# A fused attention block on one core: query and key biases carried in the first row of the weights

## The chip, the cores and the metric

The kernel runs on one core of a Trainium2 chip. Its engines work in parallel, each through its own instructions in order: TensorE (PE, with its weight loads as PEld), VectorE (DVE), ScalarE (ACT), GpSimd (POOL) and SyncE (SP), which here only issues transfers. The metric is the device time of one execution in microseconds. Three runs of the kernel before took 2831.59 to 2832.27 us, median 2831.97.

## The reference

The input is 4 batches of 1024 tokens, 512 wide. A layer norm over the 512 values gives `xn`. From it come queries, local keys and local values of 16 heads of 128 (`xn @ W + b` with `Wq`, `Wlk`, `Wlv`). Queries and keys go through an RMS norm and a rotation. Each query looks at a window of the last 128 tokens, and at the best 8 of the compressed entries (one for every 4 tokens); the mean of both goes through `Wo`. A float8 product of `xn` with `input2` and the input itself are added.

```python
xn = _layernorm(x, axis=-1)
q = (hidden_states @ Wq + bq).reshape(Bq, Sq, NH, D).transpose(0, 2, 1, 3)
q = apply_rope(rmsnorm(q, qn_w), pos)
lk = apply_rope(rmsnorm((hidden_states @ Wlk + blk).reshape(Bq, Sq, NH, D).transpose(0, 2, 1, 3), kn_w), pos)
...
merged = (ctx_sparse + ctx_local) * 0.5
x = x + (merged @ Wo + bo) + _L0_ffn_ref(xn, L0_ffn_input2, L0_ffn_scale, L0_ffn_scale1)
```

The layer norm has no weights of its own, so the 512 values of a token's `xn` sum to zero, but for rounding.

## The kernel before

The 4096 tokens are 32 blocks ("chunks" in the code) of 128 tokens, 8 to a batch. A block is done in 8 units of two heads. One loop (L791) runs over all 256 units; `s` is the unit, `t` its block and `u` its place in the block. The order on every engine is the order in which the loop body issues, written out by hand. All weights stay in SBUF.

In iteration `s` the body issues, in this order:

- the scores of unit `s` (L563: window keys, entries and a mask product on TensorE), and `keep_context` of `s-2` (ScalarE);
- `weigh` (L592) of both heads: masks, top-8 and replacement on VectorE, exponentials on ScalarE;
- `queries` (L440) of unit `s+3`: four products of 128x512 that give queries and keys of two heads (`qp`), and a fifth, in bfloat16, that adds the biases through a selecting column;
- `settle` (L623) on VectorE: choice, sums and scaling of the sparse weights;
- a first step of the generators in `running`, then the squares of `s+3` (ScalarE, L296) and from them `r`, a power on GpSimd (L290, L291);
- `settle_window` (ScalarE, L643), `to_output` of `s-2`, and a second step of the generators;
- from unit 8 on `turn` (L654): two transposes into `probB` on VectorE and a transfer to DRAM; then `values_of` (`s+1`), `normalize` (L461) of `s+3` (`th` on VectorE, a rotation half on GpSimd, `rb`, L309), the value products of `s-1`, `fetch` of the turned weights (`probT`), `turn_keys` of `s+3` with its transfers (`qk`, `qT`, `lkT`) and `keep_values` (ScalarE).

The first eight units turn weights and keys on TensorE instead (`turn_here`, `keep_turned`); their iterations also round `input2` to float8 values (units 0 to 3) and load the later weights.

Two generators run beside this, each by two steps in an iteration. `chunk_prep` of block `t+2` starts in unit 7 of block `t`: statistics (unit 7), `xn` (unit 0), its transposes `xp` and the copy `xnT` (unit 1), the product with `Wk`, `Wv` and `Wcmp` with the softmax over four tokens (units 2 and 3), entries (units 4 to 7, with a small rotation, L404 and L308, in unit 6). `chunk_eight` of block `t` starts in unit 5: `quantize` (L255) has three passes on VectorE (`qv_x`, `qm_x`) and an addition on GpSimd (L267) in its first step, then a GpSimd pass in each of the next three; the float8 product `fp` follows on TensorE in unit 7, and `f` and its addition to the input in that unit's second step.

PSUM tiles of tag `pp` (`xp`, `yp`, `ep`, `cp` of the entries, `fp`, `vp`, `tp`) share two buffers, and `scratch` (`xn`, `y`, `qv`, `qm`, `f`) shares two in SBUF. Each output of a block is finished by `x_sum` (L762) in unit 1 of the next block.

Of the kernel before, what the change touches and what calls it, by code (L numbers as in the profile page):

```python
# [12 lines left out]
F32 = mybir.dt.float32  # L13
BF16 = mybir.dt.bfloat16
U32 = mybir.dt.uint32
AF = mybir.ActivationFunctionType
ALU = mybir.AluOpType
AX = mybir.AxisListType

P = 128  # L20
# [18 lines left out]
def kernel(  # L39
# [26 lines left out]
    nc = tc.nc  # L66
    B, S, HID = hidden.shape
    NH = Wq.shape[1] // D
    KK = HID // P
    NCH = S // P  # L70
    NU = NH // 2
    NE = P // RATIO
    NT = B * NCH
# [12 lines left out]
    def scratch(name, shape=(P, 512), dtype=F32):  # L86
        return work.tile(list(shape), dtype, tag="scratch", name=name, bufs=2)
# [157 lines left out]
    def late_constants():  # L245
# [6 lines left out]
        nc.tensor.transpose(bp[:, 0:NH], blv_n, ident[:NH, :NH])  # L252
        nc.scalar.activation(blvT, bp[:, 0:NH], AF.Copy, scale=0.5)

    def quantize(dst, src, scalar, tag, m=None):  # L255

        v = scratch(f"qv_{tag}") if tag[0] == "x" else src
        if m is None:  # L260
            m = scratch(f"qm_{tag}")
        nc.vector.tensor_scalar(v, src, scalar, None, ALU.mult)
        nc.vector.tensor_scalar(
            m.bitcast(U32), v.bitcast(U32), 0x7F800000, None, ALU.bitwise_and
        )
        nc.vector.tensor_scalar(m, m, FP8_MIN_NORMAL, 1.5 * 2.0**20, ALU.max, ALU.mult)
        nc.gpsimd.tensor_tensor(v, v, m, ALU.add)  # L267
        yield
        nc.gpsimd.tensor_tensor(v, v, m, ALU.subtract)
        yield  # L270
        nc.gpsimd.tensor_scalar(m, v, FP8_OVERFLOW, 0.0, ALU.mult, ALU.mult)
        yield
        nc.gpsimd.tensor_tensor(dst, v, m, ALU.add)
        yield
# [43 lines left out]
    def chunk_prep(t):  # L318

        b, c = divmod(t, NCH)  # L320
        xt = x_tiles.pop(("norm", t))
        if c == 0:
            entries[b] = (
                work.tile([P, 2 * P], F32, tag="ckT", name=f"ckT_{b}"),
                work.tile([P, 2, D], F32, tag="cv", name=f"cv_{b}"),
            )
        ckT, cv = entries[b]
        st = work.tile([P, 8], F32, tag="lnst", name=f"lnst_{t}")
        nc.vector.bn_stats(st[:, 0:6], xt)
        nc.vector.bn_aggr(st[:, 6:8], st[:, 0:6])  # L330
        r = rstd_of(st[:, 7:8], 1, 1.0, EPS_LN, f"lnr_{t}")
        yield "A0"
        if c == 0:
            nc.gpsimd.memset(cv, 0.0)
        yield "B0"
        xn = scratch(f"xn_{t}")
        nc.vector.tensor_scalar(xn, xt, st[:, 6:7], r, ALU.subtract, ALU.mult)
        yield "A1"
        yield "B1"
        xp = pp(f"xp_{t}")  # L340
        for k in range(KK):
            nc.tensor.transpose(xp[:, ts(k, P)], xn[:, ts(k, P)], ident)
        yield "A2"
        xnT = work.tile([P, KK, P], F32, tag="xnT", name=f"xnT_{t}")
        nc.scalar.copy(xnT.rearrange("p k s -> p (k s)"), xp)
        chunks[t] = xnT
        yield "B2"


        yp = pp(f"yp_{t}")  # L350
        for k in range(KK):
            nc.tensor.matmul(
                yp[:, 0 : 2 * D + 1],
                xnT[:, k, :],
                wkv_sb[:, k, :],
                start=(k == 0),
                stop=(k == KK - 1),
            )
        yield "A3"
        y = scratch(f"y_{t}")[:, 0 : 2 * D + 1]  # L360
        nc.scalar.copy(y[:, 0 : 2 * D], yp[:, 0 : 2 * D])
        nc.gpsimd.memset(y[:, 2 * D : 2 * D + 1], 1.0)
        nc.vector.tensor_scalar(
            logits[:, 0:1], yp[:, 2 * D : 2 * D + 1], bcmp_sb, None, ALU.add
        )
        row = work.tile([P, 2, BLK], F32, tag="row", name=f"row_{t}", bufs=1)
        red = work.tile([P, BLK // RATIO], F32, tag="red", name=f"red_{t}", bufs=1)
        nc.vector.transpose(row[:, 0, :], logits)
        fours = row[:, 0, :].rearrange("p (n r) -> p n r", r=RATIO)
        nc.vector.tensor_reduce(red, fours, AX.X, ALU.max)  # L370
        nc.vector.tensor_tensor(
            fours, fours, red.unsqueeze(2).to_broadcast([P, BLK // RATIO, RATIO]), ALU.subtract
        )
        nc.scalar.activation(row[:, 0, :], row[:, 0, :], AF.Exp)
        yield "B3"
        yield "A4"
        spread_w = work.tile([P, NE], F32, tag="spread", name=f"spread_{t}", bufs=1)
        nc.vector.transpose(row[:, 1, :], row[:, 0, :])
        nc.vector.tensor_scalar(spread_w, picks, row[:, 1, 0:1], None, ALU.mult)
        yield "B4"  # L380
        ep = pp(f"ep_{t}")
        nc.tensor.matmul(ep[0:NE, 0 : 2 * D + 1], spread_w, y, start=True, stop=True)
        yield "A5"
        total = work.tile([NE, 1], F32, tag="total", name=f"total_{t}", bufs=1)
        kv = work.tile([NE, 2, D], F32, tag="kv", name=f"kv_{t}", bufs=1)
        nc.vector.reciprocal(total, ep[0:NE, 2 * D : 2 * D + 1])
        nc.vector.scalar_tensor_tensor(
            kv.rearrange("p h d -> p (h d)"),
            ep[0:NE, 0 : 2 * D],
            total,  # L390
            bkv_sb,
            ALU.mult,
            ALU.add,
        )
        yield "B5"
        g, o = divmod(c * NE, P)
        nc.scalar.copy(cv[o : o + NE, g, :], kv[:, 1, :])
        ess = work.tile([NE, 1], F32, tag="ess", name=f"ess_{t}", bufs=1)
        square_sum(ess, kv[:, 0, :], f"e{t}")
        er = rstd_of(ess, 1, 1.0 / D, EPS_RMS, f"er_{t}")  # L400
        ck = kv[:, 0:1, :]
        yield "A6"
        yield "B6"
        nc.vector.scalar_tensor_tensor(  # L404
            ck[:, 0, :], ck[:, 0, :], er, norm_w[0:NE, 1, :], ALU.mult, ALU.mult
        )
        ra = work.tile([NE, ROPE], F32, tag="ra_e", name=f"ra_e{t}", bufs=1)
        rotate(ck, angles[t][1], 1, ra, f"e{t}")
        yield "A7"
        yield "B7"  # L410
        cp = pp(f"cp_{t}")
        nc.tensor.transpose(cp[:, 0:NE], ck[:, 0, :], ident[:NE, :NE])
        yield "A8"
        nc.vector.tensor_copy(ckT[:, ts(c, NE)], cp[:, 0:NE])  # L414
        yield "B8"

    def chunk_eight(t):

        xt, xnT = x_tiles["sum", t], chunks[t]
        x8 = work.tile([P, KK * P], BF16, tag="x8", name=f"x8_{t}", bufs=1)  # L420
        src = xnT.rearrange("p k s -> p (k s)")
        yield from quantize(x8, src, scales[:, 0:1], f"x_{t}")
        fp = pp(f"fp_{t}")
        for k in range(KK):
            nc.tensor.matmul(
                fp, x8[:, ts(k, P)], w2_sb[:, k, :], start=(k == 0), stop=(k == KK - 1)
            )
        yield
        f = scratch(f"f_{t}")
        nc.vector.scalar_tensor_tensor(f, fp, inv, bo_sb, ALU.mult, ALU.add)  # L430
        nc.gpsimd.tensor_tensor(xt, xt, f, ALU.add)
# [8 lines left out]
    def queries(n):  # L440
        t, u = place(n)
        xnT = chunks[t]
        qp = psum.tile([P, 512], F32, tag="qp", name=f"qp_{n}")
        for k in range(KK):
            nc.tensor.matmul(qp, xnT[:, k, :], wqk_sb[u][:, k, :], start=(k == 0), stop=False)  # L445
        nc.tensor.matmul(
            qp, sel[:, u : u + 1].to_broadcast([P, P]), bias_b, start=False, stop=True
        )
        ss = work.tile([P, 4], F32, tag="ss", name=f"ss_{n}")
        units[n] = {"qp": qp, "ss": ss}  # L450

# [326 lines left out]
    def for_unit(n, *todo):  # L778
        if 0 <= n < NN:
            for f, *more in todo:  # L780
                f(n, *more)
# [9 lines left out]
    for s in range(-3, NN + 2):  # L791
        t, u = place(s)
# [2 lines left out]
            running = [*running[-2:], chunk_prep(t + 2)]  # L795
        if u == 3 and 0 <= t < NT:
            load_x(t, "sum")
        if u == 5 and 0 <= t < NT:
            running = [*running[-2:], chunk_eight(t)]
        if u == 4 and 0 <= t and t + 2 < NT:  # L800
            load_x(t + 2, "norm")
# [32 lines left out]
        if s + 3 >= NU:  # L834
            for_unit(s + 3, (turn_keys,), (fetch_keys,))
        for_unit(s + 1, (keep_values,))
        if s < NU:

            if s == -1:
                late_constants()  # L840
                for k in range(KK):
                    nc.scalar.dma_start(w2_raw[k], input2[ts(k, P), :])
            if 0 <= s < KK:
                for _ in range(4):
                    next(rounding, None)
            if 3 <= s + 6 < NU:
                load_wqk(s + 6, nc.scalar)
            if 3 <= s + 4 < NU:
                load_wlv(s + 4, nc.scalar)
            if 0 <= s + 1 < NU:  # L850
                load_wo(s + 1, nc.scalar)
# [49 lines left out]
```

## Time and profile before

| what | value |
|---|---|
| median of 3 runs | 2831.97 us |
| the profiled execution | 2833.53 us |
| its span, first to last instruction | 2831.6 us |
| mean granted TensorE clock | 0.997 |
| busy: PE, DVE, ACT, POOL | 2769.0, 2247.1, 1299.1, 821.3 us |
| products of `queries` (L445), busy | 945.5 us |
| transfers, mean | 141 GB/s |

Busy time is the time in which an engine has an instruction at work; idle time before an instruction is put down to what ended it. A row of the time line gives start, duration, engine, line, operation and tiles, a count where several rows are merged, and in brackets the idle time before it with its cause. Rows of one engine overlap by some tenths of a microsecond, so what an instruction costs its engine is the distance to the next start, and not its duration. Some matmul rows are missing from the trace: of the 256 bias products it has 59, while all 256 of their weight loads are there.

### The profile page before, as it was taken

The numbers are of one execution on the slowest core, as the hardware profiler recorded it, in microseconds if no ns is written. First come the engines' busy times: TensorE is split into PE (matmuls) and PEld (weight loads), VectorE is DVE, ScalarE is ACT, GpSimd is POOL, SyncE is SP. The second block draws the span as 40 slices with busy tenths as digits, with TensorE's granted clock in tenths as the row PEclk, the third lists the DMA queues.
The fourth block names the chain that finished last, engine by engine and source line by source line (L and its number), as shares of the span: only waits on it lengthen the run. The fifth ranks groups of instructions, "written<-read, shape, count | busy, mean of one in ns | idle before, by whom it ended". The sixth has DMA issues, their size and how long they took to land. (4 is left out here: it accounts for less than half of the span.)

```text
span 2831.6 us, 48506 instructions
## 1 busy us (share of the span) xinstructions
PE 2769.0 (98%) x12771; PEld 1873.8 (66%) x12969; DVE 2247.1 (79%) x9132; ACT 1299.1 (46%) x5075; POOL 821.3 (29%) x1161
## 2 busy tenths in 40 slices
PE   6999999999999999999999999999999999999998
PEld 4666666666666666666666666666666666667666
DVE  5777888888777778888877787888887777888886
ACT  3445444444444454444444444444444444444443
POOL 3432232322233322233223333223222233322221
PEclk9999999999999999999999999999999999999999
DMA  7345455555445445555544444555554544555553
GB/s 230 90 138 138 133 143 152 144 150 153 127 124 139 137 133 152 144 151 149 149 126 131 134 135 134 155 148 149 146 149 122 135 136 131 136 152 155 143 149 108
DMA packets 620850, 399.85 MB, mean 141 GB/s; under 512 B 306880, under 2 KB 573984, under 8 KB 620576
## 3 DMA queue, kind: packets, MB, share of 16 engines
q1 hardware_dynamic: 608352, 383.18, 48.8%
q10 hardware_dynamic: 12224, 13.56, 1.5%
q8 instruction: 105, 1.72, 0.3%
q14 instruction: 169, 1.38, 0.2%
HBM read 212.53 MB, written 184.03 MB: 140 GB/s over the span
## 5 line engine op out<-in xcount | busy, mean ns | idle before, releaser
L445 PE MATMUL qp<-wqk,xnT 128*128 128x512 f32 x2048 | 945.5, 604 | 4.9 <-DMA scales<-in_L_ffn_scale_dram 3.3
L445 PEld LDWEIGHTS qp<-wqk,xnT 128*128 128x128 f32 x2048 | 370.6, 191 | 385.2 <-issue 371.5
L612 ACT ACTIVATE prob<-sc,neg 128x256 f32<-128x256 f32 (+1 forms) x512 | 236.0, 461 | 779.6 <-DVE taken L611 759.3
L537 PEld LDWEIGHTS vp<-wlv,xnT 128*128 128x128 f32 x2048 | 386.5, 190 | 188.7 <-issue 94.0
L537 PE MATMUL vp<-wlv,xnT 128*128 128x256 f32 x2048 | 487.0, 381 | 17.2 <-DVE ckT L414 11.9
L753 PE MATMUL op<-wo,cT 128*128 128x512 f32 x1024 | 484.9, 596 | 7.1 <-ACT cT L735 1.5
L290 POOL TENSOR_SCALAR r<-ss 128x4 f32<-128x4 f32 x256 | 49.8, 194 | 1067.3 <-ACT junk L296 1059.3
L661 DVE STREAM_TRANSPOSE probB<-prob 128x512 f32<-128x512 f32 (+2 forms) x494 | 282.4, 609 | 92.5 <-ACT prob L643 89.1
L467 DVE SCALAR_TENSOR_TENSOR th<-qp,r,norm_w 128x128 f32<-128x128 f32 x1024 | 283.6, 339 | 71.0 <-POOL r L291 70.2
L309 POOL TENSOR_TENSOR rb<-th,cs 128x256 f32<-128x256 f32 x256 | 247.0, 965 | 278.0 <-DVE th L467 277.9
L296 ACT ACTIVATE junk<-qp 128x128 bf16<-128x128 f32 x1024 | 284.1, 277 | 88.0 <-remote 42.7
L549 ACT COPY lv<-vp 128x256 f32<-128x256 f32 x256 | 95.5, 373 | 477.6 <-PE cp L720 420.0
L753 PEld LDWEIGHTS op<-wo,cT 128*128 128x128 f32 x1024 | 188.9, 190 | 188.4 <-issue 113.9
L720 PE MATMUL cp<-probT,lv 128*128 128x128 f32 x1920 | 299.4, 276 | 4.4 <-DMA probT<-pr 4.4
L720 PEld LDWEIGHTS cp<-probT,lv 128*128 128x128 f32 x1920 | 276.1, 193 | 18.1 <-issue 5.2
L291 POOL TENSOR_TENSOR r<-r,nhalf 128x4 f32<-128x4 f32 x256 | 259.6, 1014 | 21.4
L720 PE MATMUL cp<-probT,cv 128*128 128x128 f32 x1536 | 256.7, 276 | 0.0
L582 PE MATMUL sc<-ckT,qT 128*128 128x96 f32 (+7 forms) x1024 | 226.5, 303 | 0.0
L643 ACT ACTIVATE prob<-prob,tot 128x256 f32<-128x256 f32 (+1 forms) x512 | 223.0, 484 | 3.6 <-DVE tot L637 3.6
L720 PEld LDWEIGHTS cp<-probT,cv 128*128 128x128 f32 x1536 | 214.3, 193 | 0.0
L605 DVE CUSTOM_DVE_ANT_0 sc<-sc,mask_b 128x256 f32<-128x256 f32 (+1 forms) x512 | 202.6, 396 | 7.2 <-PE sc L583 6.6
L579 PE MATMUL sc<-lkT,qT 128*128 128x128 f32 x1024 | 207.8, 285 | 0.0
(123 smaller groups left out, 3858.3 us busy)
## 6 DMA issues: line engine op xcount, KB each, us to landing
pr<-probB SPq DMA_DIRECT2D x127, 512.0 KB, 2.6
probT<-pr SPq DMA_DIRECT2D x508, 128.0 KB, 2.9
qk<-thb SPq DMA_DIRECT2D x992, 64.0 KB, 2.0
pr<-probB SPq DMA_DIRECT2D x96, 384.0 KB, 2.6
probT<-pr SPq DMA_DIRECT2D x384, 96.0 KB, 2.4
qT<-qk SPq DMA_DIRECT2D x248, 128.0 KB, 2.3
lkT<-qk SPq DMA_DIRECT2D x248, 128.0 KB, 2.5
x_norm<-_attn_hidden_states_dram SPq DMA_DIRECT2D x32, 256.0 KB, 3.2
```

The costliest lines, as they stand in the source:

```text
L291: nc.gpsimd.tensor_tensor(r, r, nhalf[: ss.shape[0], 0:n], ALU.pow)
L296: nc.scalar.activation(junk[: src.shape[0]], src, AF.Square, accum_out=acc)
L309: nc.gpsimd.tensor_tensor(bb, x12, wide(cs[:, HALF:ROPE]), ALU.mult)
L445: nc.tensor.matmul(qp, xnT[:, k, :], wqk_sb[u][:, k, :], start=(k == 0), stop=False)
L467: nc.vector.scalar_tensor_tensor(th[:, i, :], qp[:, ts(i, D)], r[:, i : i + 1], norm_w[:, i // 2, :], ALU.mult, ALU.mult,)
L537: nc.tensor.matmul(vp[:, 0:256], xnT[:, k, :], wlv_sb[u][:, k, :], start=(k == 0), stop=(k == KK - 1),)
L582: nc.tensor.matmul(sc[:, spa], q, ckT[:, 0:m], start=True, stop=False)
L612: nc.scalar.activation(prob[:, loc], sc[:, loc], AF.Exp, bias=neg[:, 0:1], scale=-1.0, accum_out=tot[:, 0:1],)
L643: nc.scalar.mul(prob[:, loc], prob[:, loc], tot[:, 0:1])
L661: nc.vector.transpose(pb[:, :, ds(h * g, g), :], prob[:, parts[0] * P : (parts[-1] + 1) * P].rearrange("p (g b i) -> p b g i", b=NB, i=BLK),)
L720: nc.tensor.matmul(blocks(cp[:, h, :]), v, probT[:, :, h * len(parts) + i - parts[0], :], start=(i == parts[0]), stop=(i == parts[-1]),)
L753: nc.tensor.matmul(op, cT[:, h, :], wo_sb[u][:, h, :], start=(u == 0 and h == 0), stop=(u == NU - 1 and h == 1),)
```

## The change

The biases are no longer added by a product of their own, from block 1 on. As the values of `xn` sum to zero, subtracting the first row of `Wq` and `Wlk` from all their rows leaves the product as it is and makes the first row zero. While block 0 is in work, iteration `s` does this for the weights of unit `s`: one VectorE subtraction over 128x2048, with the row spread over the partitions by a transfer into `probB`'s memory. Then the biases are written into the empty row by two transfers of 1 KB. The token side needs a one at that place: `xnT` gets a fifth block, a copy of the first whose first row is set to one, and blocks from 1 on use it for the first of the four products. Block 0 keeps the bias product.

As the sum must now be zero more exactly, the mean is taken off twice: ScalarE subtracts it in place and sums what is left, and `xn` subtracts the mean of that. `xn` moves a step later within unit 0. The float8 generator starts in unit 6 and not in unit 5, so its product and `f` fall in unit 0 of the next block.

```diff
+    first_row = {}
+    def load_first_row(u):
+        row = work.tile([P, 1024], F32, tag="probB", name=f"first_row_{u}", bufs=1)[:, 0:512]
+        for i, w in enumerate((Wq, Wlk)):
+            nc.sync.dma_start(row[:, ts(i, 256)], w[0, ts(u, 256)].partition_broadcast(P))
+        first_row[u] = row
+    def fold_first_row(u):
+        w = wqk_sb[u]
+        nc.vector.tensor_tensor(
+            w, w, first_row.pop(u).unsqueeze(1).to_broadcast([P, KK, 512]), ALU.subtract
+        )
+        for i, bias in enumerate((bq, blk)):
+            nc.sync.dma_start(
+                w[0:1, 0, ts(i, 256)], bias[ts(u, 256)].partition_broadcast(1)
+            )
...
         yield "B0"
+        off = work.tile([P, 2], F32, tag="off", name=f"off_{t}")
+        nc.gpsimd.tensor_scalar(off[:, 0:1], st[:, 6:7], -1.0, None, ALU.mult)
+        nc.scalar.activation(
+            xt, xt, AF.Identity, bias=off[:, 0:1], scale=1.0, accum_out=off[:, 1:2]
+        )
+        nc.gpsimd.tensor_scalar(off[:, 1:2], off[:, 1:2], 1.0 / HID, None, ALU.mult)
+        yield "A1"
         xn = scratch(f"xn_{t}")
-        nc.vector.tensor_scalar(xn, xt, st[:, 6:7], r, ALU.subtract, ALU.mult)
-        yield "A1"
+        nc.vector.tensor_scalar(xn, xt, off[:, 1:2], r, ALU.subtract, ALU.mult)
         yield "B1"
...
-        xnT = work.tile([P, KK, P], F32, tag="xnT", name=f"xnT_{t}")
-        nc.scalar.copy(xnT.rearrange("p k s -> p (k s)"), xp)
+        xnT = work.tile([P, KK + 1, P], F32, tag="xnT", name=f"xnT_{t}")
+        nc.scalar.copy(xnT[:, 0:KK, :].rearrange("p k s -> p (k s)"), xp)
+        if t:
+            nc.scalar.copy(xnT[:, KK, :], xp[:, 0:P])
+            nc.vector.memset(xnT[0:1, KK, :], 1.0)
...
-            nc.tensor.matmul(qp, xnT[:, k, :], wqk_sb[u][:, k, :], start=(k == 0), stop=False)
-        nc.tensor.matmul(
-            qp, sel[:, u : u + 1].to_broadcast([P, P]), bias_b, start=False, stop=True
-        )
+            nc.tensor.matmul(
+                qp,
+                xnT[:, k if k or not t else KK, :],
+                wqk_sb[u][:, k, :],
+                start=(k == 0),
+                stop=(t > 0 and k == KK - 1),
+            )
+        if not t:
+            nc.tensor.matmul(
+                qp, sel[:, u : u + 1].to_broadcast([P, P]), bias_b, start=False, stop=True
+            )
...
-        if u == 5 and 0 <= t < NT:
+        if u == 6 and 0 <= t < NT:
             running = [*running[-2:], chunk_eight(t)]
...
         for_unit(s + 1, (keep_values,))
+        if 0 <= s < NU:
+            fold_first_row(s)
+        if 0 <= s + 1 < NU:
+            load_first_row(s + 1)
```

More of the change, by code (lines that the diff above doesn't have):

```diff
@@ L420, in chunk_eight @@
         x8 = work.tile([P, KK * P], BF16, tag="x8", name=f"x8_{t}", bufs=1)
-        src = xnT.rearrange("p k s -> p (k s)")
+        src = xnT[:, 0:KK, :].rearrange("p k s -> p (k s)")
         yield from quantize(x8, src, scales[:, 0:1], f"x_{t}")
```

## The prediction

> **What bounds the kernel now.** I read the page first, then the list of waits, then the time line of TensorE, and last one steady token block unit by unit. A unit is two heads of a block of 128 tokens; eight make a block, 32 blocks the kernel.
>
> ```profile
> PE 2769.0 (98%) x12771; PEld 1873.8 (66%) x12969; DVE 2247.1 (79%) x9132; ACT 1299.1 (46%) x5075; POOL 821.3 (29%) x1161
> ```
> TensorE works 98% of the span. The removed product's price is the distance of starts:
>
> ```profile
> 1525.72 3.68 PE L445 MATMUL qp<-wqk,xnT 128*128 128x512 f32 x8
> 1529.24 0.38 PE L446 MATMUL qp<-bias_b,sel 128*128 128x512 bf16 x1
> 1529.45 0.60 PE L342 MATMUL xp<-ident,xn 128*128 128x128 f32 x4
> ```
> The row says 0.38, but the next product starts 0.215 us later (0.215 to 0.216 wherever a transpose or an output product follows it). 248 of 256 go: 53.4 us.
>
> That is a gain only if nothing else is nearly as slow. Below are units 1, 5 and 6 of block 4 and the sum of its eight, as VectorE walks them (first local mask L605 to that of the next unit):
>
> ```profile
> 391.30:401.91 10.61, 10.61 (x55) 7.53 (x55) 8.79 (x35) 5.33 (x20) 2.17 (x3) 1.00 0.60 174
> ...
> 435.26:447.51 12.25, 12.20 (x60) 8.46 (x61) 9.60 (x37) 5.67 (x22) 5.77 (x7) 1.00 0.47 130
> 447.51:458.28 10.77, 10.72 (x52) 7.49 (x52) 9.38 (x39) 4.86 (x19) 4.32 (x6) 1.00 0.51 148
> ...
> sum 88.22, PE 87.66 PEld 60.38 DVE 72.44 ACT 40.96 POOL 25.18; mean PE 10.96 PEld 7.55 DVE 9.05 ACT 5.12 POOL 3.15
> ```
> Columns: stretch, length, then busy time of PE, weight loads, DVE, ACT, POOL, the granted clock (1.00), DMA. TensorE idles 0.56 of 88.22 us; VectorE has 15.8 idle. Is that room? The waits say whom it waits for:
>
> ```profile
> ACT prob L612 <- DVE taken L611: 759.3, 488, 4.7
> ...
> DVE th L311 <- POOL rb L309: 159.1, 256, 0.6
> ...
> DVE probB L661 <- ACT prob L643: 89.1, 120, 1.5
> ...
> DVE th L467 <- POOL r L291: 70.2, 92, 3.2
> ...
> DVE logits L363 <- ACT y L361: 57.2, 31, 5.9
> DVE x_sum L762 <- PE op L753: 43.4, 32, 6.6
> ```
> Nearly all are waits for ScalarE or GpSimd, which themselves wait for VectorE (first line). So there is a ring: mask and top-8 (DVE), exponentials, squares, window scaling (ACT), r (POOL), th (DVE), rb (POOL), th, next unit. Only x_sum, and squares that find their product unfinished, wait for TensorE. In block 4 I take these out: without x_sum's 0.77 us and ScalarE's gaps of 0.20, 0.73 and 0.45 us ahead of the squares in units 2 to 4, units 1 to 4 are 0.56, 0.29, 0.82 and 0.61 us shorter (each then runs from its exponentials on without a gap). The ring alone then takes 85.9 us, TensorE 87.7. The same over blocks 1 to 30 (128.68 to 2734.41 us, 86.86 a block): ring 84.15. **VectorE's ring is within 3% of being the bound**; what the change adds to it decides.
>
> **The change part by part.** Block 4 is the worked case.
>
> *Bias products:* TensorE needs 87.66 - 8 x 0.2155 = 85.9 us. The move of the float8 product out of unit 7 also ends the wait there of vp for a bank that VectorE empties (ckT, 11.7 us over 17 blocks, 0.39 a block): mean need 86.86 - 1.72 - 0.39 = 84.75.
>
> *Float8 rounding from unit 5 to unit 6.* Today in unit 5:
>
> ```profile
> 440.83 0.43 DVE L266 TENSOR_SCALAR qm_x<-qm_x 128x512 f32<-128x512 f32 x1
> ...
> 441.40 1.27 POOL L267 TENSOR_TENSOR qv_x<-qv_x,qm_x 128x512 f32<-128x512 f32 x1 [0.57 <-DVE qm_x L266]
> ...
> 442.75 0.20 POOL L290 TENSOR_SCALAR r<-ss 128x4 f32<-128x4 f32 x1
> ...
> 444.08 1.12 DVE L467 SCALAR_TENSOR_TENSOR th<-qp,r,norm_w 128x128 f32<-128x128 f32 x4 [0.83 <-POOL r L291]
> ```
> L267 stands ahead of r on GpSimd, so th starts 2.82 us after qm_x ends. Without it unit 5 falls back to its squares (late by the cv copy and junk_e, 0.8): 12.2 to 10.95, -1.24. Unit 6 has the kv rotation ahead (L404 to L312, 1.43 us); then 1.39 of rounding ends at 7.38 us into the unit and th starts at 10.20, not 7.33: +2.85. The trace holds this very pile-up once, in block 0, where kv work falls in unit 5:
>
> ```profile
> 100.18 0.33 DVE L404 SCALAR_TENSOR_TENSOR kv<-kv,er,norm_w 32x128 f32<-32x128 f32 x1
> ...
> 102.17 0.43 DVE L266 TENSOR_SCALAR qm_x<-qm_x 128x512 f32<-128x512 f32 x1
> ...
> 105.42 1.13 DVE L467 SCALAR_TENSOR_TENSOR th<-qp,r,norm_w 128x128 f32<-128x128 f32 x4 [2.50 <-POOL r L291]
> ```
> Again 2.82 us after qm_x. Unit 7 keeps its length without f (0.74): its th waits for r behind lnr, not for f.
>
> *Second centring, unit 0.* ScalarE's 128x512 pass stands ahead of the squares. Rows: L612 takes 0.368 us at 128 columns, 0.474 at 256, so 0.69 at 512. ScalarE has no gap there in block 4, and f moves into this unit beside it: +0.69. Bounds: 0 (f and xn alone), 0.88 (with an accumulator read of 0.19). GpSimd's two 128x1 steps (0.19 each, as lnr's first) fit before r and ahead of xn.
>
> *Extra copy and row of ones, unit 1.* The memset waits on VectorE for ScalarE's copy and holds probB and th behind it:
>
> ```profile
> 396.70 0.69 DVE L762 TENSOR_TENSOR x_sum<-x_sum,op 128x512 f32<-128x512 f32 x1 [0.77 <-PE op L753]
> 396.98 0.57 ACT L345 COPY xnT<-xp 128x512 f32<-128x512 f32 x1
> ```
> xnT ends 6.25 us into the unit (probB starts at 6.00 today, at 397.30); a 128-column copy adds 0.17 (0.27, from 0.373 at 256 and 0.572 at 512, less 0.10 overlap), the memset 0.15 (rows: 0.06 at 4 columns, 0.27 at 256). probB can start at 6.6 against 5.4 for the ring alone: +1.16. Bounds +0.6 (x_sum waiting as now) to +1.4.
>
> Block 4: 85.91 + 0.69 + 1.16 - 1.24 + 2.85 = 89.37, against 88.22 now and 85.9 for TensorE. So the ring takes over. Done alike for blocks 1 to 30: +0.4 to +1.2 each, -0.4 in blocks 8, 16, 24; ring 87.48, **sum +18.6**.
>
> *Folding, block 0.* One 128x2048 subtraction per unit ends each unit on VectorE. TENSOR_TENSOR rows: 0.425 us at 256 columns (L310), 0.69 at 512 (L762); on that line 2.25 at 2048, bounds 2.1 and 2.75. In block 0 TensorE already waits for VectorE (vp for the lkT copy, 1.60 and 1.38 us) and VectorE's masks never for TensorE, so nothing hides it: 18.0. The rounding's move is -3.2 + 2.2 there, the first memset +0.3: **+17.2**. The 16 row loads and 16 bias loads on SP wait for a fold and are needed 10 and 50 us later; the queue's typical landing is 2 to 3 us, so 0. What stands behind them on SP, qk from unit 5 on, waits no longer than the fold.
>
> *Start.* xn now follows pass 0.69, GpSimd 0.2, and ScalarE's first pass starts only after the table load (10.55): first product at 14.1 for 11.19, **+2.9** (bounds 1.2, as the second product waits for weights until 19.86 anyway, and 3.5).
>
> *End.* Block 31 has no kv work: ring 10.5 a unit where TensorE took 10.92, for five units, and unit 5's probB 0.9 earlier: **-4**.
>
> Sum: 2.9 + 17.2 + 18.6 - 4 = +34.7 on the profiled 2833.5 (span 2831.6 and 1.9 around), 2868; on the median of 2831.97, which stands 1.6 lower: **2867**.
>
> [...] VectorE is 82% busy in block 4 (72.44 of 88.22), yet its ring leaves 2.3 us. [...]
>
> **Rivals.** (1) TensorE stays the bound, the other side: -53.4 - 11.7 + 2.9 + 14.3 (block 0 less 3 us of lead) = -48, 2784. It decides if the ring grows by under 0.6 us a block (84.15 to 84.75) where I find 3.3. For it: 98% busy. Against: the 2.82 us chain seen twice. (2) The additions on ScalarE hide (units 0 and 1 cost nothing): ring +1.61, a block 1.1 shorter than now; -33 + 16 = -17, 2815. For it: x_sum's wait stands just there. Against: x_sum no longer waits once TensorE leads. (3) TensorE cannot run ahead, since values wait for probT through DRAM, and its waits stay in the ring: another 1 us a block, 2897. Against: probT comes 7.9 us after pr, some 3 us earlier than squares need.
>
> **Numbers.** Chances: forecast 0.70, rivals 0.10, 0.12, 0.08. The forecast's own range, 0.5 us a block and the bounds of fold and start either way, is 2848 to 2888; with rival 2, 2812 to 2888. 0.2% (5.7 us) is about what a measurement tells from no change: faster 0.19, within 0.05, slower 0.76.
>
> **What would show it.** TensorE's share near 95%, with waits for probT or for score banks in every block; x_sum no longer waiting; th waiting some 1.5 us for r in unit 6 and hardly in unit 5; memset waiting for ScalarE in unit 1; folds of 2.25 us; block 4 near 89.4 us. I am wrong if TensorE's idle stays under 80 us, or th in unit 6 starts before 9 us into the unit.

## The result and the profile after

The changed kernel takes 2869.74 us (median of 4 runs, 2867.53 to 2871.94) against 2832.09 us before (median of 4, 2831.59 to 2832.27): 1.0133 times as long, 95% interval 1.0116 to 1.0151. The forecast was 2867. Its profiled execution has a span of 2867.3 us, 35.7 us more than before.

The first line of the page lists busy times and shares of the span:

```profile
PE 2759.9 (96%) x12721; PEld 1851.3 (65%) x12721; DVE 2264.2 (79%) x9171; ACT 1277.3 (45%) x5170; POOL 829.5 (29%) x1225
```

TensorE issues 248 products fewer, and its idle time rises from 62.6 to 107.4 us. The list of waits (engine, line, whom it waited for: us in total, times, longest) says where:

```profile
DVE th L506 <- POOL r L313: 100.1, 77, 2.7
...
DVE xnT L377 <- ACT xnT L376: 38.5, 31, 1.4
...
PE sc L621 <- DVE ckT L446: 28.1, 26, 2.4
PE cp L759 <- DMA probT<-pr: 24.9, 36, 2.4
...
DVE x_sum L801 <- PE op L792: 5.5, 2, 5.2
```

VectorE's wait for TensorE is all but gone (x_sum: 43.4 us before). In its place th waits longer for r (70.2 us before), and the memset of the row of ones waits for ScalarE's copy, which is new. TensorE now waits for what VectorE makes: ckT, and the weights that come back through DRAM as probT. Units 1, 5 and 6 of block 4 and the sum of its eight units, in the same columns as in the prediction:

```profile
420.58:431.71 11.13, 11.13 (x56) 7.73 (x55) 8.82 (x36) 5.34 (x21) 2.18 (x3) 1.00 0.56 166
...
463.29:474.26 10.97, 10.37 (x51) 7.13 (x50) 8.21 (x35) 5.65 (x22) 2.90 (x5) 1.00 0.62 183
474.26:487.88 13.62, 13.62 (x59) 8.47 (x59) 10.61 (x41) 4.85 (x19) 5.59 (x7) 1.00 0.49 139
...
sum 89.24, PE 88.64 PEld 60.23 DVE 72.26 ACT 40.74 POOL 25.23; mean PE 11.08 PEld 7.53 DVE 9.03 ACT 5.09 POOL 3.15
```

This stretch holds two float8 products on TensorE, the last block's in unit 0 and, issued early, its own in unit 7; the busy 88.64 us is therefore not the work of one block. What the blocks need on TensorE is seen better in e11 below, which takes 84.72 us a block with almost no idle time of TensorE. The lengths unit by unit (forecast: the prediction's own terms, applied to the lengths before):

| unit of block 4 | before | forecast | after |
|---|---|---|---|
| 0 (ScalarE's pass) | 10.02 | 10.71 | 10.72 |
| 1 (memset) | 10.61 | 11.21 | 11.13 |
| 2 | 11.82 | 11.53 | 11.51 |
| 3 | 10.87 | 10.05 | 10.03 |
| 4 | 10.66 | 10.05 | 10.03 |
| 5 (rounding gone) | 12.25 | 11.01 | 10.97 |
| 6 (rounding) | 10.77 | 13.62 | 13.62 |
| 7 | 11.22 | 11.22 | 11.22 |
| sum | 88.22 | 89.4 | 89.2 |

The time line of unit 6 shows the pile-up (start, duration, engine, line, operation and tiles, idle time before with its cause):

```profile
480.79 0.43 DVE L288 TENSOR_SCALAR qm_x<-qm_x 128x512 f32<-128x512 f32 x1
...
481.37 1.28 POOL L289 TENSOR_TENSOR qv_x<-qv_x,qm_x 128x512 f32<-128x512 f32 x1 [1.78 <-DVE qm_x L288]
...
483.01 1.02 POOL L313 TENSOR_TENSOR r<-r,nhalf 128x4 f32<-128x4 f32 x1
...
484.06 1.13 DVE L506 SCALAR_TENSOR_TENSOR th<-qp,r,norm_w 128x128 f32<-128x128 f32 x4 [1.62 <-POOL r L313]
```

From the end of the last rounding pass (481.22) to th (484.06) are 2.84 us; the forecast took 2.82 from two older places. Unit 1 shows the memset, waiting for ScalarE with probB behind it:

```profile
425.14 0.68 DVE L801 TENSOR_TENSOR x_sum<-x_sum,op 128x512 f32<-128x512 f32 x1
...
426.73 0.27 ACT L376 COPY xnT<-xp 128x128 f32<-128x128 f32 x1
...
427.08 0.17 DVE L377 MEMSET xnT<- 1x128 f32 x1 [1.26 <-ACT xnT L376]
427.17 1.23 DVE L700 STREAM_TRANSPOSE probB<-prob 128x512 f32<-128x512 f32 x2
```

### The profile page after: what moved, and what is told of

Its sections match the earlier page's. It is cut to its first block, busy times and chain, and to the rows that moved or that the text cites. A ratio compares the mean times of both kernels' runs of the same rounds, so it can differ in the third digit from the quotient of the medians.

```text
span 2867.3 us, 48457 instructions
## 1 busy us (share of the span) xinstructions
PE 2759.9 (96%) x12721; PEld 1851.3 (65%) x12721; DVE 2264.2 (79%) x9171; ACT 1277.3 (45%) x5170; POOL 829.5 (29%) x1225
## 5 line engine op out<-in xcount | busy, mean ns | idle before, releaser
L759 PE MATMUL cp<-probT,lv 128*128 128x128 f32 x1920 | 305.1, 279 | 30.5 <-DMA probT<-pr 24.9
L759 PEld LDWEIGHTS cp<-probT,lv 128*128 128x128 f32 x1920 | 267.6, 192 | 69.9 <-issue 52.5
L621 PE MATMUL sc<-ckT,qT 128*128 128x96 f32 (+7 forms) x1024 | 230.1, 307 | 28.1 <-DVE ckT L446 28.1
L333 DVE TENSOR_TENSOR th<-thb,rb 128x128 f32<-128x128 f32 x256 | 87.2, 341 | 156.3 <-POOL rb L331 155.7
```

The lines of the kernel that those rows point to most:

```text
L621: nc.tensor.matmul(sc[:, spa], q, ckT[:, 0:m], start=True, stop=False)
L759: nc.tensor.matmul(blocks(cp[:, h, :]), v, probT[:, :, h * len(parts) + i - parts[0], :], start=(i == parts[0]), stop=(i == parts[-1]),)
```

## The experiments

The theory is that of the prediction: in the changed kernel VectorE's ring sets the time of a block, and its length is the sum of the listed steps. The main rival is that TensorE still sets it and the loss lies elsewhere. "A block" below is the mean over blocks 1 to 30, from the first local mask of unit 8 to that of unit 248, divided by 30; it is 86.86 us before and 87.41 after. Differences to the changed kernel are taken from its 2869.74 us; the kernel before stood at 2831.6 to 2833.2 us beside the three groups of runs, e1 to e4, e5 to e8 and e9 to e12, so that they hold to some 2 us. The first local mask comes between 46.8 and 47.9 us in the kernels that start alike (the changed one, e1 to e4 and e6), so a difference of under 1 us there means nothing.

**The bias product issued again (e1).**

```diff
-            nc.vector.memset(xnT[0:1, KK, :], 1.0)
+            nc.vector.memset(xnT[0:1, KK, :], 0.0)
...
-                stop=(t > 0 and k == KK - 1),
-            )
-        if not t:
-            nc.tensor.matmul(
-                qp, sel[:, u : u + 1].to_broadcast([P, P]), bias_b, start=False, stop=True
-            )
+                stop=False,
+            )
+        nc.tensor.matmul(
+            qp, sel[:, u : u + 1].to_broadcast([P, P]), bias_b, start=False, stop=True
+        )
```

> The changed kernel with the bias product of every block issued again (the row of ones is then a row of zeros, so that the bias is not added twice). Theory (VectorE's ring sets the time, 87.41 us a block measured over blocks 1 to 30): TensorE's need grows by 8 x 0.2155 = 1.72 to about 86.5 us a block, still under the ring in nearly every block, so little shows: 2870 to 2885 us. Rival (TensorE sets the time): 248 x 0.2155 = 53 us come back, 2918 to 2926.

Measured: 2868.71 us (2866.87 to 2871.96), the same as without the product and 1 us below the expected range; a block 87.42 us.

```profile
PE 2799.3 (98%) x12969; PEld 1880.8 (66%) x12969; DVE 2261.7 (79%) x9171; ACT 1286.0 (45%) x5170; POOL 829.2 (29%) x1225
```

All 248 products are back (12969 weight loads for 12721), TensorE is busy 39 us longer, and the kernel is not a microsecond slower. The rival expected 53 us. What the change removes is worth nothing in the kernel that it makes.

**The rounding back in unit 5 (e2).**

```diff
-        if u == 6 and 0 <= t < NT:
+        if u == 5 and 0 <= t < NT:
             running = [*running[-2:], chunk_eight(t)]
```

> The changed kernel with the float8 rounding back in unit 5. Theory: unit 6 of a block loses its 2.85 us and unit 5 gains 1.24 to 1.28, 1.6 a block over 30 blocks: -48, which leaves the ring at 85.8, just above what TensorE needs (84.75, and 0.39 of it comes back with the wait for ckT's bank): 2815 to 2832, about 2822. Rival (the ring is not the bound): 2864 to 2876, no change.

Measured: 2834.29 us (2831.56 to 2836.85), 35 us less than the changed kernel, though 48 were expected, and 2 above the expected range; a block 86.13 us, not 85.8. The rival (no change) is out. Most of the missing part lies where one wait of TensorE has grown, before (first) and in e2 (second):

```profile
PE vp L537 <- DVE ckT L414: 11.9, 18, 1.1
```

```profile
PE vp L576 <- DVE ckT L446: 35.8, 30, 2.4
```

With the float8 product in unit 7, vp waits for one of the two `pp` buffers until VectorE has copied ckT. The wait is longer where TensorE has less other work: e8 below shows it in the kernel before (30.2 us for 11.9). In units 0 and 3 to 5 of block 4 the squares then come late again, for a product unfinished.

**Only GpSimd's addition moved behind r, rounding still in unit 6 (e3).**

```diff
+        if tag[0] == "x":
+            yield
         nc.gpsimd.tensor_tensor(v, v, m, ALU.add)
-        yield
+        if tag[0] != "x":
+            yield
         nc.gpsimd.tensor_tensor(v, v, m, ALU.subtract)
```

> The changed kernel with the rounding left in unit 6, its three VectorE passes too, and only the GpSimd addition moved from before r to behind it, into the same unit's second step. Theory (what costs in unit 6 is that the addition stands ahead of r on GpSimd): th starts at about 8.1 us into unit 6 and not at 9.8, the unit is 11.9 us and not 13.6, 1.65 x 30 = -50: 2815 to 2828. Rival (the three passes on VectorE cost it, 1.39 us a block): th stays near 9.8, 2864 to 2874.

Measured: 2826.58 us (2823.37 to 2828.51), 43 us less than the changed kernel, and 0.998 of the kernel before (0.9971 to 0.9989). The time line of unit 6 of block 4, which begins at 470.44:

```profile
476.12 1.31 POOL L316 TENSOR_TENSOR r<-r,nhalf 128x4 f32<-128x4 f32 x1
...
477.31 1.30 DVE L703 STREAM_TRANSPOSE probB<-prob 128x512 f32<-128x512 f32 x2
...
477.54 1.28 POOL L291 TENSOR_TENSOR qv_x<-qv_x,qm_x 128x512 f32<-128x512 f32 x1
...
478.53 0.57 DVE L509 SCALAR_TENSOR_TENSOR th<-qp,r,norm_w 128x128 f32<-128x128 f32 x2
```

th (L509) starts 8.09 us into the unit without waiting, 9.80 in the changed kernel. The three VectorE passes stand where they stood, so the order on GpSimd was the cause of the wait. The unit is 12.25 us long and not the 11.9 expected; 0.37 of that is in one VectorE row, thb: 0.79 us, with GpSimd's next 128x512 pass beside it, and 0.42 before (more such rows in the last section).

**The row of ones made by GpSimd (e4).**

```diff
-            nc.scalar.copy(xnT[:, KK, :], xp[:, 0:P])
-            nc.vector.memset(xnT[0:1, KK, :], 1.0)
+            nc.gpsimd.tensor_scalar(xnT[:, KK, :], xnT[:, 0, :], 1.0, None, ALU.mult)
+            nc.gpsimd.memset(xnT[0:1, KK, :], 1.0)
```

> The changed kernel with the extra block of xnT and its row of ones made by GpSimd out of xnT, so that no VectorE instruction waits for ScalarE's copies in unit 1. Theory: probB starts in unit 1 at 5.4 us and not at 6.59, -1.1 x 30 = -33: 2830 to 2843, with x_sum still not waiting. Rival (x_sum's wait for TensorE, 0.77 us before, takes the place): half of it, 2848 to 2858. If the ring does not set the time: 2870.

Measured: 2838.40 us (2836.86 to 2840.00), -31 us; a block 86.36, unit 1 on average 9.80 us instead of 10.83. x_sum does not wait (5.9 us in the whole kernel). GpSimd's two instructions, 0.54 and 0.19 us, lie in its idle time between r and rb.

**One centring (e5).**

```diff
-        off = work.tile([P, 2], F32, tag="off", name=f"off_{t}")
-        nc.gpsimd.tensor_scalar(off[:, 0:1], st[:, 6:7], -1.0, None, ALU.mult)
-        nc.scalar.activation(
-            xt, xt, AF.Identity, bias=off[:, 0:1], scale=1.0, accum_out=off[:, 1:2]
-        )
-        nc.gpsimd.tensor_scalar(off[:, 1:2], off[:, 1:2], 1.0 / HID, None, ALU.mult)
...
-        nc.vector.tensor_scalar(xn, xt, off[:, 1:2], r, ALU.subtract, ALU.mult)
+        nc.vector.tensor_scalar(xn, xt, st[:, 6:7], r, ALU.subtract, ALU.mult)
```

> The changed kernel without the second centring: ScalarE's pass and GpSimd's two small steps are left out, and xn subtracts the first mean (its sum is then zero only to the rounding of one mean). Theory: unit 0 loses 0.69 us in 30 blocks, -21, and the start some 3 to 4: 2842 to 2850. Rival (ScalarE's pass lies beside VectorE's work): only the start, 2865 to 2868.

Measured: 2850.13 us (2849.36 to 2850.47), -20 us, at the upper end of the expected range: the first local mask comes at 42.28 us instead of 46.83 (-4.6), block 0 is 1.0 shorter, and a block is 86.97 (-0.44, 13 in all). Unit 0 of block 4 is 10.27 us, with the pass 10.72, before 10.02. So taking the pass out gives back 0.45 of the 0.70. What is left belongs to f, not to xn: with the rounding moved and xn in its old place (e7) the unit takes 10.27 us too, and with xn a step later and f still in unit 7 (e10) it takes 10.03. In the changed kernel f is hidden beside the pass, for probB waits there for ScalarE and not for VectorE (first row); in e5 it follows xn at once (second):

```profile
415.97 1.30 DVE L700 STREAM_TRANSPOSE probB<-prob 128x512 f32<-128x512 f32 x2 [0.36 <-ACT prob L682]
```

```profile
408.39 1.30 DVE L694 STREAM_TRANSPOSE probB<-prob 128x512 f32<-128x512 f32 x2
```

**No folds (e6).**

```diff
-        nc.vector.tensor_tensor(
-            w, w, first_row.pop(u).unsqueeze(1).to_broadcast([P, KK, 512]), ALU.subtract
-        )
+        first_row.pop(u)
```

> The changed kernel without the eight subtractions of 128x2048 in block 0 (the first row's share of queries and keys is then missing from block 1 on); its transfers stay. Theory: 8 x 2.25 = 18 us, and some 3 to 4 more that block 0 showed above that (in its units 1 and 3 TensorE's granted clock was 0.88 and 0.79): 2845 to 2853. Rival (the transfers are what lengthens block 0): 2862 to 2870.

Measured: 2851.30 us (2850.73 to 2853.79), -18 us; block 0 takes 89.66 us instead of 108.00, the other blocks the same 87.41. The 18.3 us of block 0 are not a clean price: unit 0 of e6 takes 15.63 us (14.09 in the changed kernel, 12.31 before) at a granted clock of 0.75, with ScalarE idle for 8.2 us behind its loads of weights (4.7 in the changed kernel), and no run shows whether the transfers that stay have a part in that. In units 1 to 7 the folds are worth 19.9 us, and units 1 and 3 are back at 11.16 and 11.17 us as before the change.

**The kernel before, with only the rounding moved (e7).**

```diff
-        if u == 5 and 0 <= t < NT:
+        if u == 6 and 0 <= t < NT:
             running = [*running[-2:], chunk_eight(t)]
```

> The kernel before with nothing changed but the start of the float8 rounding, unit 6 for unit 5. Theory: the ring grows by 1.6 to 85.8 us a block, but TensorE, with the bias product still there, needs 86.86 - 0.39 = 86.5, so the time stays about: 2820 to 2840. Rival (each us in the ring is a us of time, before as after): +48, 2870 to 2885.

Measured: 2815.99 us (2811.68 to 2817.84), ratio 0.9940 (0.9925 to 0.9955): 17 us faster than before, 4 below the expected range. A block is 86.46 us, and 86.86 - 0.39 = 86.47 was the prediction's figure for TensorE without the bank wait; 12 us come from there and 3 from the last block. Unit 6 is as long as in the changed kernel (13.61 us in block 4), and here it costs nothing: TensorE idles less than before (14.9 us after block 0, 26.9 before), and the other units together are shorter by more than this one is longer. In the changed kernel undoing this edit gains 35 us (e2), in the one before making it gains 17.

**The kernel before without the bias product (e8).**

```diff
-            nc.tensor.matmul(qp, xnT[:, k, :], wqk_sb[u][:, k, :], start=(k == 0), stop=False)
-        nc.tensor.matmul(
-            qp, sel[:, u : u + 1].to_broadcast([P, P]), bias_b, start=False, stop=True
-        )
+            nc.tensor.matmul(qp, xnT[:, k, :], wqk_sb[u][:, k, :], start=(k == 0), stop=(t > 0 and k == KK - 1))
+        if not t:
+            nc.tensor.matmul(
+                qp, sel[:, u : u + 1].to_broadcast([P, P]), bias_b, start=False, stop=True
+            )
```

> The kernel before with the bias product left out from block 1 on and nothing put in its place (queries and keys lack their bias there). Theory (TensorE is the bound before, the ring 2.7 us a block below it): TensorE's need falls to 85.14 us a block, the ring alone takes 84.15, so nearly all 53 us are gained: 2780 to 2795. Rival (the ring binds already before): 2810 to 2832.

Measured: 2798.85 us (2797.96 to 2799.63), 34 us under before, between the two expectations. A block is 85.76 us, where TensorE would need 85.14: the bank wait of vp grew here too, from 11.9 to 30.2 us. So even with nothing put in its place the product is worth 34 of its 53 us.

**All additions taken off the ring (e9), with three variants.** e9 joins e3 and e4 and two edits more: ScalarE's centring pass goes behind the window scaling in unit 7, and GpSimd does the folds of units 4 to 7.

```diff
-        nc.vector.tensor_tensor(
+        (nc.gpsimd if u > 3 else nc.vector).tensor_tensor(
             w, w, first_row.pop(u).unsqueeze(1).to_broadcast([P, KK, 512]), ALU.subtract
...
+        off = work.tile([P, 2], F32, tag="off", name=f"off_{t}")
+        nc.scalar.activation(
+            xt, xt, AF.Identity, bias=st[:, 6:7], scale=-1.0, accum_out=off[:, 1:2]
+        )
         yield "B0"
...
-        off = work.tile([P, 2], F32, tag="off", name=f"off_{t}")
-        nc.gpsimd.tensor_scalar(off[:, 0:1], st[:, 6:7], -1.0, None, ALU.mult)
-        nc.scalar.activation(
-            xt, xt, AF.Identity, bias=off[:, 0:1], scale=1.0, accum_out=off[:, 1:2]
-        )
         nc.gpsimd.tensor_scalar(off[:, 1:2], off[:, 1:2], 1.0 / HID, None, ALU.mult)
+        nc.gpsimd.tensor_scalar(off[:, 0:1], r, -1.0, None, ALU.mult)
...
-        nc.vector.tensor_scalar(xn, xt, off[:, 1:2], r, ALU.subtract, ALU.mult)
+        nc.vector.tensor_scalar(xn, xt, off[:, 1:2], off[:, 0:1], ALU.subtract, ALU.mult)
```

> The changed kernel with its additions taken off the ring: the rounding's addition behind r (as in e3), the row of ones by GpSimd (as in e4), ScalarE's centring pass moved from ahead of the squares in unit 0 to behind the window scaling in unit 7, and the folds of units 4 to 7 on GpSimd. Theory: from e3's 86.0 us a block go 1.03 (unit 1, measured in e4) and 0.6 (unit 0), ring 84.3; TensorE needs 84.75 and sets the time again; with 0.4 for an uneven block 85.2 x 30, 66 us under the changed kernel, and 9 us less for four folds: 2788 to 2803. Rival (the ring's savings do not add up): 2805 to 2820.

Measured: 2795.38 us (2794.03 to 2800.20), ratio to before 0.9872 (0.9858 to 0.9887). A block is 84.82 us, TensorE's need being 84.75, with 14 us of idle time of TensorE in all of units 8 to 255 (gaps over 0.06 us; 62 in the changed kernel). The fold's part failed: block 0 takes 113.9 us, 6 more than in the changed kernel (last section).

e10 is e9 with the rounding in unit 5 (the edit of e2).

> As e9, but the rounding in unit 5. Theory: the ring is shorter still (in unit 5 the rounding's passes lie beside probB's wait for late squares, 1.71 us in block 4), but vp waits in unit 7 again for the bank that VectorE empties (36 us in e2), so TensorE needs 85.1 to 85.9: 2795 to 2815, not below e9. Rival (only the ring's length counts): 10 to 20 us below e9.

Measured: 2822.74 us (2822.05 to 2823.52), 27 us above e9 and 8 above its range; a block 85.61. The bank wait is there:

```profile
PE vp L579 <- DVE ckT L449: 27.5, 30, 1.8
```

Units 5 and 6 of block 4 together are 0.6 us shorter than in e9 and no more, since GpSimd's addition and subtraction now stand ahead of rb in unit 5 (12.12 us). Units 1 to 4 lose 1.3 us: behind the bank wait TensorE comes late to them, the squares wait for an unfinished product (20.9 us over the kernel, 3.9 in e9) and x_sum waits again (31.8 us, 5.2 in e9). The rival, by which only the ring's length counts, is out.

e11 is e9 with the layer norm's power behind r in unit 7:

```diff
+        yield "A0"
         r = rstd_of(st[:, 7:8], 1, 1.0, EPS_LN, f"lnr_{t}")
-        yield "A0"
```

> As e9, and in unit 7 the power for the layer norm (lnr) goes behind r on GpSimd, so that th no longer waits 1.05 us for r there. Theory: the ring loses 1 us a block more; as TensorE should be the bound in e9 already, at most 5 to 10 us: 2780 to 2800. If e9 is still bound by the ring: 25 to 30 us below e9.

Measured: 2787.99 us (2786.54 to 2792.11), ratio to before 0.9848 (0.9832 to 0.9864), 44 us less than before and the fastest run here. th waits for r for 8.2 us in the whole kernel (46.1 in e9), and a block takes 84.72 us. Blocks gain 0.1 and not 1 us each against e9, as they do when TensorE is the bound; of the 12.3 us between the two profiled spans 6.7 lie in block 0.

e12 is e9 with the bias product issued again, by the edit of e1.

> As e9, with the bias product of every block issued again (and the row of ones a row of zeros), the same edit as e1. Theory: with the ring at 84.3, TensorE's need of 84.75 + 1.72 = 86.5 us sets the time and the product that cost nothing in e1 costs 1.2 to 1.7 us a block: 35 to 50 us above e9, 2825 to 2845. Rival (the product's time is hidden whatever the ring does): within 5 us of e9.

Measured: 2842.78 us (2841.66 to 2843.34), 47 us above e9; a block 86.23, that is 1.41 more of the product's 1.72. The 248 products are back here as in e1, and TensorE is busy 50 us longer than in e9 (first row: e9):

```profile
PE 2737.9 (98%) x12721; PEld 1855.8 (66%) x12721; DVE 2284.0 (82%) x9136; ACT 1301.8 (47%) x5139; POOL 881.2 (32%) x1291
PE 2788.3 (98%) x12969; PEld 1880.9 (66%) x12969; DVE 2287.5 (81%) x9136; ACT 1316.0 (46%) x5139; POOL 884.5 (31%) x1291
```

The same edit as in e1 costs 47 us here and nothing there. This is the pair on which the verdict rests.

## Why the prediction was right

The sum by places, from the two traces (first local mask of unit 0, of unit 8, of unit 248, end):

| term | forecast, us | measured, us |
|---|---|---|
| start, to the first mask | +2.9 | 46.83 - 41.46 = +5.4 |
| block 0 | +17.2 | 108.00 - 87.23 = +20.8 |
| blocks 1 to 30 | +18.6 | 2622.23 - 2605.73 = +16.5 |
| block 31 and end | -4 | 90.24 - 97.14 = -6.9 |
| sum | +34.7 | +35.7 |

- **The ring and not TensorE.** Right: e1 against e12. TensorE was 98% busy before and stays at 96%, and the 53 us of its products are worth nothing until the ring is shortened.
- **Unit 6, +2.85.** The length is right to 0.01 us, and the addition ahead of r is the main cause (e3). The exactness is luck, for two sizes were off and cancel. The rounding ends 6.96 us into the unit and not at 7.38, so th starts at 9.80 and not at 10.20; from th to the end of the unit it takes 3.82 us and not 3.43 as before. Both come from a later GpSimd pass of the rounding (the one that makes qm_x), of whose effect the prediction says nothing. Before, it stood in unit 6 beside a row of the kv rotation, which then took long (first two rows). Moved along with the rounding, it now stands beside a row of the rotation of th, which now takes long (last two).

```profile
452.82 0.61 POOL L271 TENSOR_SCALAR qm_x<-qv_x 128x512 f32<-128x512 f32 x1
452.88 0.59 DVE L311 TENSOR_TENSOR kv<-ra_e,rb_e 32x32 f32<-32x32 f32 x1 [0.23 <-POOL rb_e L309]
```

```profile
486.20 0.62 POOL L293 TENSOR_SCALAR qm_x<-qv_x 128x512 f32<-128x512 f32 x1
486.26 0.69 DVE L333 TENSOR_TENSOR th<-thb,rb 128x128 f32<-128x128 f32 x1 [0.62 <-POOL rb L331]
```

  Without the pass beside them, the kv row takes 0.18 us (after) and the th row 0.29 (before): 0.41 less, 0.40 more.
- **Unit 1, +1.16.** Measured +1.08 in block 4; e4 gives back 1.03 on average. Rival 2, in which this hides, falls with it: x_sum no longer waits. But the reason given, that x_sum stops waiting because TensorE leads, is not what the runs show: without the bias product and with the rounding in its old place (e8) x_sum still waits 32.1 us, and with the product and only the rounding moved (e7) 5.2. It is the move of the rounding, and with it of the float8 product out of unit 7, that ends this wait.
- **Unit 0, +0.69.** Right (+0.70), with f hidden beside the pass as assumed. Only the lower bound, 0 for f and xn alone, was too low: without the pass 0.25 stays (e5).
- **Units 2 to 5.** Right to 0.04 us each: units 2 to 4 fall to the ring's own length once TensorE leads, as the prediction took them.
- **Block 0.** The folds are 2.28 us each, forecast 2.25. Left out was what they do to TensorE: in units 1 and 3 it idles 3.7 and 3.9 us where it idled 1.4 and 1.0, its granted clock over the unit is 0.88 and 0.79 where it was 1.00, and the units grow by 3.6 and 5.3 us with the fold in them (without the folds, e6, by nothing).
- **Start.** The first product starts at 13.77 us, forecast 14.1. Missed was that block 1 is centred too before the loop reaches unit 0:

```profile
38.70 0.21 POOL L360 TENSOR_SCALAR off<-lnst 128x1 f32<-128x1 f32 x1
38.95 0.72 ACT L361 ACTIVATE x_norm<-x_norm,off 128x512 f32<-128x512 f32 x1 [1.13 <-POOL off L360]
...
39.67 0.26 ACT L318 ACTIVATE junk<-qp 128x128 bf16<-128x128 f32 x1
```

  The squares wait 1.13 us for GpSimd and 0.72 for the pass. The centring is 4.6 us of the start (e5), where 2.9 was forecast.
- **The bank wait in unit 7.** Taken out with its 0.39 us a block, right for the kernel before (e7: 86.46 for 86.47). It is no constant: 11.9 us before, 30.2 in e8, 35.8 in e2. The prediction did not see that the move of the rounding could gain 17 us by itself.
- **What would show it.** Right: x_sum, th in units 5 and 6 (1.0 and 53.3 us over the kernel), the memset, the folds, block 4, TensorE's share (96%, forecast near 95). Wrong in part: TensorE waits for probT (24.9 us) and, where score banks were named, for ckT in its scores (28.1), in about one unit of a block and not throughout. Rival 3, by which such waits add another microsecond to each block, is out: a block takes 87.41 us, forecast 87.48.

The start and block 0 came out 6.1 us too small and the other two terms 5.0 too large, so part of the exactness of the sum is luck. The last block takes between 89.2 and 93.0 us in the changed kernel, e4, e5 and e6, which have the same work there, so 2 or 3 us of its term mean nothing.

## What to carry to other kernels

An engine that is 98% busy can be within 3% of not being the bound: before pricing work taken from it, add up the longest ring of waits through the other engines, and price what the edit adds to that ring. The test is cheap: issue the removed work again, and if the time stays, the gain was never there. An instruction that is cheap on its own engine (GpSimd's 1.27 us addition, whose move gained 43 us in e3) is dear where a short one that the ring needs stands behind it; its place in the order, not its engine's load, is what to change.

## What the runs showed of the hardware

**TensorE's clock fell after 3.7 us of idling, and sometimes after less.** TensorE's rows of vp in units 1 and 3 of block 0 of the changed kernel, and then those of unit 1 before:

```profile
66.66 3.41 PE L576 MATMUL vp<-wlv,xnT 128*128 128x256 f32 x8 [3.70 <-DVE lkT L536]
...
94.50 3.78 PE L576 MATMUL vp<-wlv,xnT 128*128 128x256 f32 x8 [3.88 <-DVE total L418]
```

```profile
59.52 1.99 PE L537 MATMUL vp<-wlv,xnT 128*128 128x256 f32 x8 [1.38 <-DVE lkT L497]
```

The same eight products take 1.99 us after 1.38 us of idling, 3.41 after 3.70 and 3.78 after 3.88; the granted clock over the two units is 0.88 and 0.79, and 1.00 in the same units before. The granted clock of the 4 us after the two longer waits is 0.64 and 0.50. A shorter idling was not always harmless: in the changed kernel TensorE idles 2.40 us ahead of 404.23 and 2.43 ahead of 2834.01, and the granted clock of the next 4 us is 0.59 and 0.57. It idles 1.99 us ahead of 1467.72, that clock is 0.66, and the eight products of `queries` there take 5.38 us; it idles 2.07 us ahead of 1016.33, the clock is 1.00, and they take 3.68. What decides between the last two no run here shows. So a wait that VectorE imposed on TensorE cost more here than its own length: over units 1 and 3 TensorE idles 2.3 and 2.9 us more than before, and the units are 3.6 and 5.3 us longer.

**A VectorE instruction was held for the whole of a GpSimd pass.** In e9, with the fold on GpSimd:

```profile
112.33 4.50 POOL L269 TENSOR_TENSOR wqk<-wqk,first_row 128x2048 f32<-128x2048 f32 x1
112.40 4.57 DVE L336 TENSOR_TENSOR th<-thb,rb 128x128 f32<-128x128 f32 x1 [0.62 <-POOL rb L334]
```

L336 takes 0.29 us in most units; here it begins 0.07 us after the fold and ends 0.14 us after it. Each of the four folds holds one such row, of 4.57, 4.58, 3.59 and 4.58 us. So a fold moved to idle GpSimd held VectorE some 4 us where VectorE's own fold takes 2.28: block 0 of e9 is 6 us longer, not 9 shorter. What holds it no run here shows. The same shows small in unit 6, before and after (the rows shown with the prediction's unit 6: 0.59 us for 0.18, and 0.69 for 0.29), and in e3 and e10, where a 0.42 us product of VectorE (thb, the rotation) took 0.79 and 1.46 us beside GpSimd's passes. Not every VectorE row is held: beside e4's 0.54 us pass the two transposes into probB took 1.30 us together and the four rows of th 1.09, where the changed kernel's took 1.30 and 1.13 (the rows at 415.97 and 484.06 above).
